# The last stage of a one-core attention and mixture-of-experts kernel: the output normalisation block by block, with roots by GpSimd and some sums by TensorE

## The chip, the cores and the metric

The kernel runs on one core of one Trainium2 chip. The metric is the device time of one execution in microseconds (us). A profiled execution also has a span, from the first to the last instruction of the program; all times inside a profile count from the start of the span. The engines are called PE (TensorE), DVE (VectorE), ACT (ScalarE), POOL (GpSimd) and SP (SyncE, which here only issues DMAs).

## The reference, cut to what matters

The input x is 4 x 1024 rows of 256 floats. After an attention layer with 16 heads comes a mixture of 8 experts, of which each row uses two; both layers stand between layer normalisations, and all is float32:

```python
x = x + _layernorm(_L0_attn_ref(_layernorm(x, axis=-1), ...), axis=-1)
x = x + _layernorm(_L0_ffn_ref(_layernorm(x, axis=-1), ...), axis=-1)
...
def _layernorm(x, axis=-1, eps=1e-05):
    m = jnp.mean(x, axis=axis, keepdims=True)
    v = jnp.var(x, axis=axis, keepdims=True)
    return (x - m) / jnp.sqrt(v + eps)
...
        h = jax.nn.silu(xs @ Wg[e] + bg[e]) * (xs @ W1[e] + b1[e])
        out = out + we[:, e:e + 1] * (h @ W2[e] + b2[e])
```

The change touches the last line of the first extract alone: the sum of a row's two weighted expert results, its layer normalisation, and the addition to the residual.

## The kernel before, in words

The attention fills the first two thirds of the span, with PE, DVE and ACT all at work; POOL takes part in the rotary embedding, in the small root calculations and in sending rows to their experts. Then the expert stage runs over 46 tiles of 256 or 128 rows. For each tile PE multiplies, ACT applies silu, DVE multiplies and scales (`up`, `down`), and POOL sends the weighted result by an indirect DMA (line 1276) to the DRAM tensor `res`, which has a place for the first and for the second expert's result of each row. PE's `pu` tiles of this stage lie in the PSUM pool `psu`, which has five buffers of one bank each.

When all results have landed, the end begins. The 4096 rows are eight blocks of 512. A block is an SBUF tile of 128 partitions, each with four rows; the four rows of a partition are called four tiles `t`.

1. `results` (line 1293) loads both results of each block into a tile `a` of its own: `a[:, 0]` on SP's queue, `a[:, 1]` on ACT's queue, half a megabyte each. All sixteen loads are issued first.
2. `scales_of` works on a pair of blocks: for each block DVE adds the two results (line 1302) and takes statistics of each tile (line 1304). `norm_scales` then makes mean and variance (line 358), adds eps (line 360) and calls `inverse_root`. That computes 1/sqrt(v) by an integer first guess (lines 337 and 338, always on DVE) and three Newton steps on the engine `e` it is given. On DVE a step is three instructions (lines 342 to 345), on POOL four. Two more instructions make the offset (lines 363 and 364). A root on DVE is so 11 instructions after the first guess, on POOL 14. Here `e` is DVE.
3. ACT scales each tile with the root and the offset (line 1310), from `a[:, 0]` into `a[:, 1]`.
4. `store` adds the residual (DVE, line 1317) and issues the store on SP (line 1318).

The engines SP, PE, DVE and ACT run in the order in which the program gives their instructions (a manual schedule), and POOL's instructions are kept in program order by the wrapper `InOrder` (line 328 is where they are all recorded). The order before is: statistics and roots of pair 0, of pair 1, stores of pair 0, pair 2, stores of pair 1, pair 3, stores of pair 2, stores of pair 3. The small tiles of the root (`mv`, `var`, `i`, `y`, `t`, `off`) have two buffers each.

Of the kernel before, what the change touches and what calls it, by code (L numbers as in the profile page):

```python
# [8 lines left out]
F32 = mybir.dt.float32  # L9
I32 = mybir.dt.int32  # L10
F32R = mybir.dt.float32r
AF = mybir.ActivationFunctionType
# [4 lines left out]
P = 128  # L17
B, T, C = 4, 1024, 256
# [6 lines left out]
NTB = TB // P  # L25
NBLK = B * T // TB
# [31 lines left out]
def sandwich(  # L58
# [4 lines left out]
    nc = tc.nc  # L63

    const = ctx.enter_context(tc.tile_pool(name="const", bufs=1))
    small = ctx.enter_context(tc.tile_pool(name="small", bufs=2))
# [65 lines left out]
    ident = const.tile([P, P], F32, tag="ident", name="ident")  # L132
# [34 lines left out]
    def compact():  # L167
        for i in range(2):
            for k in range(KC):
                nc.scalar.copy(  # L170
                    wqk[:, k, :, i],
                    w2x[:, i * KC + k, :].rearrange("p (g h d) -> p g h d", h=4, d=32)[..., :HD],
                )
# [117 lines left out]
    for e in range(NE):  # L291
        for w, to, cols in (
            (wg, 0, slice(0, FF)), (w1, FF, slice(FF - (P - R2), FF)), (w1, FF + P - R2, slice(0, NC * P))
        ):
            n = cols.stop - cols.start
# [34 lines left out]
    pool = InOrder(nc.gpsimd)  # L330

    def inverse_root(v, shape, name, e):

        i = small.tile(shape, I32, tag=f"ir{name[0]}", name=f"i_{name}")
        y = small.tile(shape, F32, tag=f"rt{name[0]}", name=f"y_{name}")
        t = small.tile(shape, F32, tag=f"rr{name[0]}", name=f"t_{name}")
        nc.vector.tensor_scalar(i, v.bitcast(I32), 1, None, ALU.arith_shift_right)
        nc.vector.tensor_scalar(  # L338
            y.bitcast(I32), i, -1.0, float(0x5F3759DF), ALU.mult, ALU.add
        )  # L340
        for _ in range(3):
            e.tensor_tensor(t, y, y, ALU.mult)
            if e is nc.vector:
                e.scalar_tensor_tensor(t, t, -0.5, v, ALU.mult, ALU.mult)
                e.scalar_tensor_tensor(y, t, 1.5, y, ALU.add, ALU.mult)
            else:
                e.tensor_tensor(t, t, v, ALU.mult)
                e.tensor_scalar(t, t, -0.5, 1.5, ALU.mult, ALU.add)
                e.tensor_tensor(y, y, t, ALU.mult)
        return y  # L350

    def norm_scales(stats, n, name, e=None):


        e = e or pool
        mv = small.tile([P, n, 2], F32, tag=f"mv{name[0]}", name=f"mv_{name}")
        for t in range(n):
            nc.vector.bn_aggr(mv[:, t, :], stats[:, t, :])
        v = small.tile([P, n], F32, tag=f"var{name[0]}", name=f"var_{name}")
        nc.vector.tensor_scalar(v, mv[:, :, 1], EPS, None, ALU.add)  # L360
        rstd = inverse_root(v, [P, n], name, e)
        off = small.tile([P, n], F32, tag=f"off{name[0]}", name=f"off_{name}")
        e.tensor_tensor(off, mv[:, :, 0], rstd, ALU.mult)
        e.tensor_scalar(off, off, -1.0, None, ALU.mult)
        return mv, rstd, off

    def normalized(out, src, scales, t):
        _, rstd, off = scales
        nc.scalar.activation(
            out, src, AF.Identity, bias=off[:, t : t + 1], scale=rstd[:, t : t + 1]  # L370
        )
# [5 lines left out]
    def stats_tile(name):  # L377
        return small.tile([P, NTB, 6], F32, tag=f"st{name[0]}", name=f"st_{name}")
# [19 lines left out]
    def bank_free(r, n):  # L398
        return max(ring[r][(taken[r] + i) % len(ring[r])] for i in range(n))
# [56 lines left out]
    def run_one(first="PADGW"):  # L456

        w = next((w for w in works if w.need[0] in first and w.fits()), None)
        if w:
            w.run()  # L460
        return w
# [623 lines left out]
    room = {}  # L1085
# [209 lines left out]
            )  # L1295
        return a

    def scales_of(pair):

        stats = small.tile([P, 2 * NTB, 6], F32, tag="st4", name=f"sto_{pair}")  # L1300
        for i, a in enumerate(sums[2 * pair : 2 * pair + 2]):
            nc.vector.tensor_tensor(a[:, 0], a[:, 0], a[:, 1], ALU.add)  # L1302
            for t in range(NTB):
                nc.vector.bn_stats(stats[:, i * NTB + t, :], a[:, 0, t, :])  # L1304
        scales = norm_scales(stats, 2 * NTB, f"o{pair}", nc.vector)
        for i, a in enumerate(sums[2 * pair : 2 * pair + 2]):
            for t in range(NTB):
                _, rstd, off = scales
                n = slice(i * NTB + t, i * NTB + t + 1)
                nc.scalar.activation(  # L1310
                    a[:, 1, t, :], a[:, 0, t, :], AF.Identity, bias=off[:, n], scale=rstd[:, n]
                )

    def store(blk, q):
        b, t0 = blk // 2, (blk % 2) * TB
        a = sums[blk]
        nc.vector.tensor_tensor(a[:, 1], a[:, 1], xs[blk], ALU.add)  # L1317
        q.dma_start(
            out=out[b, t0 : t0 + TB, :].rearrange("(p t) c -> p t c", p=P), in_=a[:, 1]
        )  # L1320

    sums, xs = [], []
# [29 lines left out]
    with tc.manual_schedule(engines={ET.SP, ET.PE, ET.DVE, ET.Activation}):  # L1352

        starts = [prepare(0, h, x_first[h], fast=True) for h in range(NQB)]
        for k in range(20):
            for gen in starts:
                next(gen, None)
            if k == 4:
                compact()
                small_constants()  # L1360
            if k == 8:
                turned_constants()
        plan_stacks()
        for h in range(NQB):
            splitting[0, 0, h].finish()
        for h in range(NQB):
            stacking[0, 0, h].finish()
        for t in range(NT):
            pressing.append(Work(values(0, [t]), t - 1))
        late = [Work(late_constants(), 40), Work(biases_by_chunk(), 57, start=54)]  # L1370
        while drawn[0] < UNIT:
            if bank_free("D", 2) <= free["P"]:
                peaks()
            elif not run_one():
                free["P"] = bank_free("D", 2)
        shifts[0].finish()
        for n in range(len(order) * NT):
            plan(n)
            for w in list(works):
                if w.due < n and w in pressing:  # L1380
                    w.finish()
            step(n)
            if "tb" not in room and n >= (len(order) - 4) * NT:

                if all(w.need is None for w in [*stacking.values(), *pressing]):
                    make_room_early()
                    first = Work(first_tiles(), n, after=[settling[divmod(NA - 1, NQB)]])
        while waiting:
            weighted(*waiting.pop(0))
        for to, of in bulk:  # L1390
            nc.sync.dma_start(out=to, in_=of)
        backs[-1].finish()
        first.finish()
        make_room()

        last = iter(())
        xT = transposed(0, ready[0][0])
        for j in range(MT):  # L1400
            if j == MA - 2:
                while works:
                    if not run_one():
                        free["P"] += 200
                for _ in other_tiles():
                    pass
            xt, w = ready.pop(0)
            for f in (NC, 0, 1):
                up(j, w, xT, f)
                run_one()  # L1410
            next(last, None)
            for f in (2, 3):
                up(j, w, xT, f)
                run_one()
            for _ in last:
                pass
            if j + 2 < MT:
                ready.append(fetch(j + 2))
            if j + 1 < MT:
                nxt = transposed(j + 1, ready[0][0])  # L1420
            up(j, w, xT, 4)
            xT, last = nxt, down(j, xt, w)
            if MA <= j < MA + NBLK:

                blk = j - MA
                xb = room["hp"].tile([P, NTB, C], F32, tag=f"x{blk}", name=f"x_{blk}")
                nc.sync.dma_start(
                    out=xb, in_=resid[blk * TB : (blk + 1) * TB, :].rearrange("(p t) c -> p t c", p=P)
                )
                xs.append(xb)  # L1430
        for _ in last:
            pass
        weights.close()
        open_pool("lp", behind, bufs=1, side="right")
        for blk in range(NBLK):
            sums.append(results(blk))
        for pair in range(NBLK // 2 + 1):
            if pair < NBLK // 2:
                scales_of(pair)
            if pair:  # L1440
                for i in range(2):
                    store(2 * pair - 2 + i, nc.sync)
    behind.close()


# [77 lines left out]
```

## Time and profile before

| what | value |
|---|---|
| median of 4 runs (lowest, highest) | 1680.26 us (1678.57, 1683.75) |
| the profiled execution's own time | 1680.44 us |
| its span | 1678.4 us |
| PE busy, share of the span | 1536.4 us, 92% |
| DVE busy | 1062.8 us, 63% |
| ACT busy | 853.7 us, 51% |
| POOL busy | 507.2 us, 30% |
| DMA, mean over the span | 147 GB/s |
| last indirect DMA of `down` issued | 1622.82 |
| first load of the end issued | 1625.23 |
| end of the last DVE instruction | 1674.85 |

The shares are means over stages with different limits. The end is some 53 us of the 1678, so it is read by itself: in the timeline (instructions in order of time, with the idle time before each), in windows (busy time of each engine in a stretch, with PE's granted clock), and in groups by line. A group's row gives the line, the engine, the operation, the tiles written and read, and the count, with the shortest, the median and the longest duration.

### The profile page before, as it was taken

How to read it: one execution, taken by the hardware profiler on the slowest of the kernel's cores; microseconds unless marked ns; L12 is line 12 of the kernel's file. 1: busy time of each engine (PE TensorE's matmuls, PEld its weight loads, DVE VectorE, ACT ScalarE, POOL GpSimd, SP SyncE). 2: the span in 40 equal slices, each digit the busy share in tenths (PEclk: the TensorE clock that was granted, in tenths of full speed). 3: DMA queues.
4: the chain of work that ended last, by engine and by line, in shares of the span. 5: the costliest groups of instructions: out<-in, count | busy, mean ns of one | idle time of the engine just before them, and what ended most of it. 6: DMA issues, size and time to landing. Idle time of an engine off the chain costs nothing. (4 is left out here: it accounts for less than half of the span.)

```text
span 1678.4 us, 27338 instructions
## 1 busy us (share of the span) xinstructions
PE 1536.4 (92%) x9448; PEld 1002.5 (60%) x9448; DVE 1062.8 (63%) x2535; ACT 853.7 (51%) x1753; POOL 507.2 (30%) x915
## 2 busy tenths in 40 slices
PE   3789999999989999999999999999999999999960
PEld 2344455654545554445554444788888888888850
DVE  6558778788688788778788894334434333333338
ACT  2156677676757677667677767422221111222213
POOL 5360262065354055265144121223230111111100
PEclk8879999999999999999999999999999999999985
DMA  2549769253434351204033032245455555778755
GB/s 79 144 117 275 204 188 271 58 140 95 128 75 98 89 173 40 63 26 103 15 82 81 1 118 102 77 166 203 159 194 191 205 202 199 266 281 288 286 204 209
DMA packets 102782, 247.32 MB, mean 147 GB/s; under 512 B 14029, under 2 KB 73652, under 8 KB 96756
## 3 DMA queue, kind: packets, MB, share of 16 engines
q1 hardware_dynamic: 92404, 215.00, 41.0%
q0 software_dynamic: 8768, 25.33, 4.7%
q10 hardware_dynamic: 1472, 5.24, 0.9%
q8 instruction: 75, 1.23, 0.3%
q14 instruction: 63, 0.52, 0.1%
HBM read 148.75 MB, written 80.58 MB: 137 GB/s over the span
## 5 line engine op out<-in xcount | busy, mean ns | idle before, releaser
L672 DVE TENSOR_REDUCE part<-pm 128x1 f32<-128x512 f32 x1024 | 640.3, 681 | 154.3 <-PE pm L668 153.2
L764 ACT ACTIVATE e<-sc 128x512 f32<-128x512 f32 x1024 | 529.7, 604 | 154.5 <-PE sc L760 153.2
L1229 PE MATMUL pu<-xT,w 128*128 128x256 f32 (+3 forms) x2024 | 361.7, 332 | 3.5 <-DVE xT L1211 1.0
L1229 PEld LDWEIGHTS pu<-xT,w 128*128 128x128 f32 (+1 forms) x2024 | 313.8, 189 | 36.6 <-issue 6.0
L1235 ACT ACTIVATE sil<-pu,w 128x256 f32<-128x256 f32 (+3 forms) x276 | 117.0, 424 | 429.5 <-PE pu L1229 400.9
L668 PE MATMUL pm<-stack,stack 64*128 64x512 f32 x960 | 273.8, 468 | 28.5 <-DVE part L672 14.5
L829 PE MATMUL av<-e,v 128*32 128x512 f32 x2048 | 276.8, 610 | 0.3 <-ACT e L764 0.3
L1240 DVE SCALAR_TENSOR_TENSOR h<-pu,w,sil 128x256 f32<-128x256 f32 (+1 forms) x230 | 97.1, 423 | 220.0 <-ACT sil L1235 219.8
L668 PEld LDWEIGHTS pm<-stack,stack 64*128 64x128 f32 x960 | 133.0, 186 | 169.7 <-DVE part L672 108.4
L760 PE MATMUL sc<-shift,bring 64*128 64x512 f32 x1024 | 224.5, 400 | 0.4 <-ACT shift L657 0.2
L753 PE MATMUL sc<-stack,stack 64*128 64x512 f32 x960 | 213.9, 408 | 9.1 <-ACT half L603 7.8
L1276 POOL DMA_INDIRECT res<-yo,ids x71 | 68.8, 969 | 427.4 <-DVE yo L1275 426.0
L1263 PE MATMUL pe<-w,h 128*128 128x256 f32 x710 | 169.6, 386 | 0.0
L1263 PEld LDWEIGHTS pe<-w,h 128*128 128x128 f32 x710 | 130.9, 190 | 31.1 <-issue 15.2
L753 PEld LDWEIGHTS sc<-stack,stack 64*128 64x128 f32 x960 | 111.5, 188 | 38.3 <-ACT half L603 12.9
L760 PEld LDWEIGHTS sc<-shift,bring 64*128 64x128 f32 x1024 | 108.1, 187 | 21.3 <-ACT shift L657 5.3
L1275 DVE TENSOR_SCALAR yo<-pe,xt 128x256 f32<-128x256 f32 x71 | 34.3, 483 | 99.9 <-PE pe L1263 99.9
L829 PEld LDWEIGHTS av<-e,v 128*32 128x32 f32 x2048 | 40.9, 108 | 71.7 <-issue 66.0
L1016 POOL DMA_INDIRECT rows<-xr,to x64 | 62.6, 978 | 60.9 <-DVE to L1011 26.8
L328 POOL TENSOR_TENSOR rot<-turned,bias_qk 128x512 f32<-128x512 f32 x31 | 40.9, 1319 | 115.2 <-ACT turned L528 108.1
L328 POOL TENSOR_TENSOR t_y<-y_y 128x4 f32<-128x4 f32 x24 | 4.7, 197 | 187.3 <-DVE y_y L338 186.1
L523 PE MATMUL pp<-wqk,nT 128*128 128x512 f32 (+1 forms) x128 | 61.0, 600 | 0.0
(293 smaller groups left out, 1418.8 us busy)
## 6 DMA issues: line engine op xcount, KB each, us to landing
w<-wall SPq DMA_DIRECT2D x46, 2034.0 KB
rows<-empty SPq DMA_DIRECT2D x35, 1032.0 KB
stack<-half SPq DMA_DIRECT2D x92, 256.0 KB
stack<-half SPq DMA_DIRECT2D x64, 128.0 KB
xt<-rows SPq DMA_DIRECT2D x25, 258.0 KB
wall<-in_wg_dram SPq DMA_DIRECT2D x16, 342.0 KB
wall<-in_w_dram SPq DMA_DIRECT2D x16, 320.0 KB
wall<-in_w_dram SPq DMA_DIRECT2D x8, 640.0 KB
```

The costliest lines, as they stand in the source:

```text
L668: nc.tensor.matmul(pm, q[r, t * P : (t + 1) * P], k_[r, half * TB : (half + 1) * TB], start=True, stop=True,)
L672: nc.vector.tensor_reduce(part[:, i, 2 * pr + s, half : half + 1], pm, AX.X, ALU.max)
L753: nc.tensor.matmul(sc, k_[r, kb * P : (kb + 1) * P], q[r, qb * TB : (qb + 1) * TB], start=True, stop=False,)
L760: nc.tensor.matmul(scs[s], bring[pr][r, :], shift[u][r, :], start=False, stop=True)
L764: nc.scalar.activation(e, scs[s], AF.Exp, scale=1.0 / HD**0.5)
L829: nc.tensor.matmul(av[32 * j : 32 * j + 32, :], v_aug[kb][:, 4 * g + j, :], es[j], start=(kb == 0), stop=(kb == NT - 1),)
L1016: sent = nc.gpsimd.indirect_dma_start(out=rows[:, :], out_offset=bass.IndirectOffsetOnAxis(ap=to[:, i, t : t + 1], axis=0), in_=xr[:, t, i ...
L1229: nc.tensor.matmul(pu[:m, i, :n], w[:, c0 : c0 + m], xT[:, k, :n], start=(k == 0), stop=(k == KC - 1),)
L1235: nc.scalar.activation(sil[:m, :n], pu[:m, 0, :n], AF.Silu, bias=w[:m, OB + f : OB + f + 1])
L1240: nc.vector.scalar_tensor_tensor(h[:, f, :n], pu[:, 1, :n], bias, sil[:, :n], ALU.add, ALU.mult)
L1263: nc.tensor.matmul(po[:, :C], hs[j % 2][:, f, i * P : (i + 1) * P], w[:, O2 + f * C : O2 + (f + 1) * C], start=False, stop=(f == NC - 1),)
L1276: sent = nc.gpsimd.indirect_dma_start(out=res[:, :], out_offset=bass.IndirectOffsetOnAxis(ap=ids, axis=0), in_=y, in_offset=None,)
```

## The change

The end goes block by block. In `summed_up`, for blocks 1, 3 and 5, PE sums the two results: for each half of the block (two tiles, 512 columns) two products with the identity matrix are accumulated into a PSUM bank of the pool `psu`, and the statistics and ACT's scaling then read PSUM. For the other five blocks DVE adds as before. Each block has its own `norm_scales`; the roots of blocks 0 to 6 go to POOL, that of block 7 stays on DVE. The store of block k - 2 is placed after the statistics of block k and ahead of its aggregates and root. The last two stores follow at the end. Loads, stores and their queues are as they were.

```diff
-    def scales_of(pair):
-
-        stats = small.tile([P, 2 * NTB, 6], F32, tag="st4", name=f"sto_{pair}")
-        for i, a in enumerate(sums[2 * pair : 2 * pair + 2]):
+    def summed_up(blk):
+
+        a, by_tile = sums[blk], []
+        if blk in (1, 3, 5):
+            for n in range(2):
+                p = room["psu"].tile([P, 2, C], F32, tag="pu", name=f"sum_{blk}_{n}")
+                for i in range(2):
+                    nc.tensor.matmul(
+                        p.rearrange("p t c -> p (t c)"), ident,
+                        a[:, i, 2 * n : 2 * n + 2].rearrange("p t c -> p (t c)"),
+                        start=(i == 0), stop=(i == 1),
+                    )
+                by_tile += [p[:, 0], p[:, 1]]
+        else:
             nc.vector.tensor_tensor(a[:, 0], a[:, 0], a[:, 1], ALU.add)
-            for t in range(NTB):
-                nc.vector.bn_stats(stats[:, i * NTB + t, :], a[:, 0, t, :])
-        scales = norm_scales(stats, 2 * NTB, f"o{pair}", nc.vector)
-        for i, a in enumerate(sums[2 * pair : 2 * pair + 2]):
-            for t in range(NTB):
-                _, rstd, off = scales
-                n = slice(i * NTB + t, i * NTB + t + 1)
-                nc.scalar.activation(
-                    a[:, 1, t, :], a[:, 0, t, :], AF.Identity, bias=off[:, n], scale=rstd[:, n]
-                )
+            by_tile = [a[:, 0, t] for t in range(NTB)]
+        stats = stats_tile(f"o{blk}")
+        for t in range(NTB):
+            nc.vector.bn_stats(stats[:, t, :], by_tile[t])
+        return by_tile, stats
+
+    def scaled(blk, by_tile, scales):
+        for t in range(NTB):
+            normalized(sums[blk][:, 1, t], by_tile[t], scales, t)
...
-        for pair in range(NBLK // 2 + 1):
-            if pair < NBLK // 2:
-                scales_of(pair)
-            if pair:
-                for i in range(2):
-                    store(2 * pair - 2 + i, nc.sync)
+
+        for blk in range(NBLK):
+            by_tile, stats = summed_up(blk)
+            if blk > 1:
+                store(blk - 2, nc.sync)
+            scales = norm_scales(stats, NTB, f"o{blk}", pool if blk < NBLK - 1 else nc.vector)
+            scaled(blk, by_tile, scales)
+        for blk in (NBLK - 2, NBLK - 1):
+            store(blk, nc.sync)
```

`normalized` is the same ACT instruction that `scales_of` used, and `stats_tile` gives a tile for the statistics of four tiles.

## The prediction

> **What bounds the kernel now.** I read the page first (spans and clock), then the timeline of the last 60 us, then the waits of that stretch, then earlier stretches for the prices of what is new. The part that the change touches begins when the last results have landed in DRAM. In the timeline the columns are start, length, engine, line, operation, count, and in brackets the idle time before and what ended it.
>
> ```profile
> 1625.24 14.45 ACTq L1293 DMA_DIRECT2D a<-res  x8
> 1630.64 1.23 DVE L1302 TENSOR_TENSOR a<-a 128x1024 f32<-128x1024 f32 x1 [8.09 <-DMA a<-res]
> 1631.90 1.41 DVE L1304 BATCH_NORM_STATS2 sto<-a 128x6 f32<-128x256 f32 x4
> 1633.47 1.22 DVE L1302 TENSOR_TENSOR a<-a 128x1024 f32<-128x1024 f32 x1 [0.17 <-DMA a<-res]
> ...
> 1669.56 4.04 ACT L1310 ACTIVATE a<-a,off_o,y_o 128x256 f32<-128x256 f32 x8 [6.72 <-DVE off_o L364]
> 1673.63 1.22 DVE L1317 TENSOR_TENSOR a<-a,x 128x1024 f32<-128x1024 f32 x1 [0.72 <-ACT a L1310]
> ```
>
> The reader sees one engine: DVE starts at 1630.64 when block 0 lands and works until 1674.85 with two short waits. The windows by stage agree; their columns are busy times of PE, PEld, DVE, ACT and POOL, then clock, DMA share, GB/s:
>
> ```profile
> 1640.00:1650.00 10.00, 0.00 (x0) 0.00 (x0) 9.45 (x34) 5.74 (x12) 0.00 (x0) 0.50 0.79 313
> 1650.00:1660.00 10.00, 0.00 (x0) 0.00 (x0) 9.45 (x35) 3.29 (x8) 0.00 (x0) 0.50 0.26 104
> ```
>
> DVE is busy 9.45 of 10 us, POOL and PE not at all, and PE's granted clock has dropped to 0.50. The loads keep the DMA full (about 410 GB/s) until 1647.5, some 2.6 us a block; after that DMA is no bound. From the last add's end at 1674.85 to the span's end at 1678.4 are 3.55 us of store and shutdown, which stay. The execution's own time is 1680.44, 2.04 over its span; the median is 1680.26, so I add the difference to the median.
>
> **What leaves DVE.** By the timeline's pitches a DVE block costs: add 1.25, four statistics 1.33, four aggregates 0.33, three small operations (var, i, y) 0.60; the rest of a root 11 x 0.20 = 2.2; the result add before a store 1.19. Before: 8 x (1.25+1.33+0.33+1.19) + 4 x 14 x 0.20 = 44. After: five blocks at 1.25+1.33, three at 4 x 0.345 = 1.38 (statistics from PSUM have no row; of 128x256 operations with a PSUM input L706 took 424 ns and L1275 483, where L951 from SBUF took 425, so a tile costs 0 to 58 ns more, in all at most 0.7 us; I take 0.345 a tile, by L706, which is as much of a two-input read), eight times 0.33+0.60+1.19, one root of 2.2: 36.2. So 8 us leave DVE. I do not credit them, since three other things become late.
>
> **Late thing 1: the sums on PE.** Block 1 has four calls of 128x512. Line 194 shows that one fp32 call of that shape is two records, 1.02 us at full clock, so 0.5 a record.
>
> ```profile
> 25.79 1.02 PE L194 MATMUL pbias<-diag,ones 128*128 128x512 f32 x2
> 51.78 1.65 PE L523 MATMUL pp<-wqk,nT 128*128 128x384 f32 x2
> ...
> 53.00:54.00 1.00, 1.00 (x3) 0.50 1.05 340
> 54.00:55.00 1.00, 1.00 (x5) 0.82 1.06 329
> ```
>
> At half clock two records of 384 columns took 1.65, so one of 512 takes 1.65/2 x 512/384 = 1.1. A burst that began at 51.05 got the full clock at 54.36 (0.82 in that microsecond is 36% at 0.50), after 3.3 us. PE starts at 1633.5: three records by 1636.8, five at 0.5, and 0.15 to the reader: the second half is there at 1639.45. DVE, done with block 0 at 1634.1, takes tiles 0 and 1 at 1637.2 and the other two until 1640.15; aggregates and small operations end at 1641.1. DVE has stood still for 4.7 us. Bounds: 5.0 without any waiting (the sum could not be earlier than the load), and 6.9 when the clock stays at 0.50 for all eight records (8 x 1.1 + 0.15). Blocks 3 (landed about 1639.3) and 5 (about 1644.2) are summed long before DVE asks for them, and stay so at half clock within 1.5 us.
>
> [...]
>
> **Late thing 2: POOL is slower and is held up.** A root of 14 operations took POOL 433.24 to 437.10, 3.86 us (DVE: 2.2). It never ran beside DVE's big SBUF adds in this kernel, and the new end puts ten of those adds beside it. The nearest rows are those where both engines did two-input work in SBUF:
>
> ```profile
> 27.51 1.79 POOL L328 TENSOR_TENSOR rot<-turned,bias_qk 128x512 f32<-128x512 f32 x1 [7.00 <-ACT bias_qk L197]
> ...
> 31.10 1.59 POOL L328 TENSOR_TENSOR rot<-rot,turn 128x512 f32<-128x512 f32 x1
> ...
> 27.46 0.69 DVE L550 TENSOR_TENSOR rot<-turned,bias_qk 128x512 f32<-128x512 f32 x1 [0.79 <-ACT bias_qk L197]
> ...
> 30.48 1.09 DVE L561 TENSOR_TENSOR rot<-rot,turn 128x512 f32<-128x512 f32 x1
> ...
> L328 POOL TENSOR_TENSOR rot<-turned,bias_qk x31: 1261/1305/1789, 27.5 to 853.4; 128x512 f32<-128x512 f32 x31
> L328 POOL TENSOR_TENSOR rot<-rot,turn x31: 1260/1282/1591, 31.1 to 856.3; 128x512 f32<-128x512 f32 x31
> ```
>
> The first POOL operation began with 0.64 us of DVE's left and took 1.79 for a median 1.305: 0.48 lost, the rest less 0.16. The second had 0.47 left and lost 0.31: again the rest less 0.16. So POOL stands still while such a DVE operation runs. An add of 1.216 at some point in a chain costs it 1.216 - 0.16 - 0.05 (the gap between POOL's operations): 1.0. Bounds: 0 (none of the rows is of a 0.2 us operation behind a 1.2 us one) and 1.22. I take 1.0, since both rows give the same rule. In return DVE waits at most for the rest of a 0.2 us operation, a few hundredths. Statistics and aggregates hold nothing: roots beside L375 and L358 kept a pitch of 0.28 to 0.30.
>
> [...]
>
> **Late thing 3: one chain per block.** DVE's store add of block k-2 stands before the root of block k, so it now waits for POOL and ACT, and behind it queue the aggregates, the small operations and all later DVE work. ACT itself is free only at 1639.69 (its loads, first fence), which covers root 0. A block's scaling is four tiles: 0.585 + 3 x 0.49 = 2.1. The order from there (16xx us; POOL goes from chain to chain without a gap, since each y is ready before POOL is; a chain is 3.86 plus 1.0 for each add that falls into it):
>
> | root | POOL from | adds in it | to | scaled |
> |---|---|---|---|---|
> | 1 | 41.15 | add 2, store 0 | 47.0 | 49.1 |
> | 2 | 47.0 | store 1, add 4 | 52.9 | 55.0 |
> | 3 | 52.9 | store 2 | 57.7 | 59.8 |
> | 4 | 57.7 | store 3, add 6 | 63.6 | 65.7 |
> | 5 | 63.6 | store 4, add 7 | 69.5 | 71.6 |
> | 6 | 69.5 | store 5 | 74.3 | 76.4 |
>
> Six chains of 3.86 and ten adds of 1.0 are 33.2 us. Each store add starts when "scaled" says, so DVE idles 1 to 2 us before each. Block 7 is rooted on DVE by 1676.1 (y at 1673.8 and 2.2); ACT comes to it after block 6 and ends at 1678.4, and the last add at 1679.7. That is 4.85 after 1674.85: a span of 1683.2, the execution 1685.3, and on the median **1685.1 us**. Stores are issued on SP behind the loads (last issue 1639) and cost nothing; PE's sixth PSUM tile waits for the first to be read (five buffers), at about 1649, and block 5 is asked for at 1657.
>
> **Rivals.**
> 1. POOL and DVE don't hold each other in 0.2 us pieces. Then DVE paces: from 1641.1 blocks 2, 4, 6 at 4.7, blocks 3, 5 at 3.5, block 7 at 4.7+2.2, 28.0 in all, and 0.4 of waits: 1669.5; scaling 2.1 and the last add 1.25: 1672.9, which is 1.9 less, 1678.4. For it: small POOL operations kept their pitch beside DVE's PSUM work. Against: the rows above. It decides where a hold costs under about 0.5: each tenth less takes ten times 0.1 from the 4.85. With 0.6 to 0.8 a hold the time is 1681 to 1683.
> 2. No hold, and PE's sums ready when block 1 lands: then ACT's queue is next, store 0 can't start before 1639.7 + 2.1 = 1641.8, and y of block 2 comes at 1644.0 for 1645.8: another 1.8 less, -3.7, **faster**, 1676.5. Against: 0.50 in every window from 1625.
> 3. The clock does not rise, or holds are 1.22 each: +7.1 (the first term 2.3 later) or +7, about 1687.5.
> 4. The holds are there and PE's sums are no wait: root 1 then starts when root 0 ends (1634.2 + 3.9 = 1638.1), 3.0 sooner than in the table: +1.85, 1682.1.
>
> **Numbers.** Forecast (1683.7 to 1686.5) 0.42; rival 3 0.20; holds of 0.5 to 0.8 or rival 4 (1680.5 to 1683.6) 0.19; rival 1 0.12; rival 2 0.07. The range leaves out rival 2 and the far end of 3: 1678.3 to 1688.5. A measurement of this kernel tells about 0.2% (3.4 us) from no change. Slower by more: 0.62 and a little of the third case, 0.64; within: 0.29; faster: 0.07.
>
> **What would show it.** Right: DVE's first statistics of block 1 wait 3 to 4 us for PE, and the next pair again; POOL's root operations show lengths up to about 1.2 us, two of 14 in a chain; store adds wait for ACT by 1 to 2 us; POOL has no gap from 1641 to 1674. Wrong: roots of 3.9 us each, and DVE without gaps after 1641 (rival 1), or a clock of 1.00 before 1635 (rival 2).

## The result, and the profile after

The changed kernel takes 1684.13 us (median of 44 runs, 1681.18 to 1688.41) where the kernel before, measured beside it, takes 1680.7 us (66 runs, 1677.43 to 1688.21). The ratio is 1.0018, with a 95% interval from 1.0013 to 1.0024: slower by 2.2 to 4.0 us. The prediction took 0.2% (3.4 us) as the least that can be told from no change; the point lies just under that and the interval reaches over it, but 1.0000 lies well outside the interval.

The profiled execution took 1686.87 us, span 1685.1. Only part of that is the change: the stages ahead of it are the same code and differ by some microseconds from execution to execution (the first load of the end is issued at 1625.23 in the profile of before, at 1629.24 in this one, and at 1623.22 to 1628.04 in the profiles of e1 to e4 below). So I use one measure for all profiles, the **end stage**: from the issue of that first load to the end of the span. Before it is 1678.4 - 1625.23 = 53.2 us, after 1685.1 - 1629.24 = 55.9 us: 2.7 us longer, in agreement with the ratio (2.2 to 4.0).

The timeline after, as for before (start, length, engine, line, operation, count, idle time before it):

```profile
1634.66 1.23 DVE L1312 TENSOR_TENSOR a<-a 128x1024 f32<-128x1024 f32 x1 [8.10 <-DMA a<-res]
...
1637.01 5.10 PE L1305 MATMUL sum<-a,ident 128*128 128x512 f32 x8 [10.97 <-DMA a<-res]
...
1640.43 0.76 DVE L1316 BATCH_NORM_STATS2 st_o<-sum 128x6 f32<-128x256 f32 x2 [2.21 <-PE sum L1305]
...
1642.15 0.76 DVE L1316 BATCH_NORM_STATS2 st_o<-sum 128x6 f32<-128x256 f32 x2 [0.96 <-PE sum L1305]
...
1643.71 1.23 DVE L1312 TENSOR_TENSOR a<-a 128x1024 f32<-128x1024 f32 x1
...
1643.89 1.11 POOL L328 TENSOR_TENSOR t_o<-y_o 128x4 f32<-128x4 f32 x1 [1.71 <-DVE y_o L338]
...
1645.07 0.20 POOL L328 TENSOR_TENSOR t_o<-t_o,var_o 128x4 f32<-128x4 f32 x1
...
1646.29 1.21 DVE L1326 TENSOR_TENSOR a<-a,x 128x1024 f32<-128x1024 f32 x1
...
1646.48 1.08 POOL L328 TENSOR_SCALAR t_o<-t_o 128x4 f32<-128x4 f32 x1
...
1651.54 1.23 DVE L1326 TENSOR_TENSOR a<-a,x 128x1024 f32<-128x1024 f32 x1 [1.80 <-ACT a L369]
...
1651.74 1.08 POOL L328 TENSOR_TENSOR t_o<-y_o 128x4 f32<-128x4 f32 x1
...
1676.21 4.04 ACT L369 ACTIVATE a<-a,off_o,y_o 128x256 f32<-128x256 f32 x8 [2.78 <-POOL off_o L328]
...
1680.28 1.23 DVE L1326 TENSOR_TENSOR a<-a,x 128x1024 f32<-128x1024 f32 x1 [0.75 <-ACT a L369]
```

Three things are to be seen. DVE waits 2.21 and 0.96 us for PE's two halves of block 1. Each DVE add (1643.71, 1646.29, 1651.54) has a POOL operation beside it that takes 1.1 us instead of 0.2 and ends with the add. And DVE's add before a store waits 1.80 us for ACT, which waits for POOL. The windows (PE, PEld, DVE, ACT, POOL busy, clock, DMA share, GB/s) show the bound changing hands:

```profile
1650.00:1660.00 10.00, 1.98 (x4) 0.68 (x4) 7.16 (x23) 3.58 (x8) 7.96 (x26) 0.85 0.49 196
1660.00:1670.00 10.00, 0.00 (x0) 0.00 (x0) 7.45 (x25) 4.01 (x8) 7.95 (x27) 0.50 0.22 86
```

DVE falls from 9.45 of 10 us to 7.2 to 7.5, while POOL, idle before, works without a pause (its 0.2 us operations stand 0.28 apart, and the gaps don't count as busy). The groups of the root's tile `t_o` give the price of a hold, that is of one add beside which POOL stands still (shortest/median/longest ns):

```profile
L328 POOL TENSOR_TENSOR t_o<-y_o x21: 197/198/1222, 1638.3 to 1673.7; 128x4 f32<-128x4 f32 x21
L328 POOL TENSOR_SCALAR t_o<-t_o x21: 192/193/1078, 1638.9 to 1675.1; 128x4 f32<-128x4 f32 x21
```

Ten of POOL's 98 operations are stretched, to 1.13 us on average, each beside one of the ten adds that the prediction's table lists, and in the same order. Ten times (1.13 - 0.20) is 9.3 us of POOL standing still.

### The profile page after: what moved, and what is told of

Read it like the earlier page. It is cut to its first block, busy times and chain, and to the rows that moved or that the text cites. A ratio compares the mean times of both kernels' runs of the same rounds, so it can differ in the third digit from the quotient of the medians.

```text
span 1685.1 us, 27486 instructions
## 1 busy us (share of the span) xinstructions
PE 1553.4 (92%) x9472; PEld 1009.2 (60%) x9472; DVE 1057.1 (63%) x2511; ACT 853.8 (51%) x1753; POOL 535.7 (32%) x1013
## 3 DMA queue, kind: packets, MB, share of 16 engines
q8 instruction: 75, 1.23, 0.3%
## 5 line engine op out<-in xcount | busy, mean ns | idle before, releaser
L1016 POOL DMA_INDIRECT rows<-xr,to x64 | 62.6, 978 | 61.9 <-DVE to L1011 28.0
```

The costliest lines, as they stand in the source:

```text
L1016: sent = nc.gpsimd.indirect_dma_start(out=rows[:, :], out_offset=bass.IndirectOffsetOnAxis(ap=to[:, i, t : t + 1], axis=0), in_=xr[:, t, i ...
```

## The experiments

Theory: POOL stands still while DVE runs an add with two inputs in SBUF; this makes the chain of roots the bound, and PE's late sum of block 1 shifts its start. Rivals: the handing from engine to engine is the cost, whatever POOL's lengths; or the late sum alone; or POOL is slowed by any DVE work. All lengths are of the end stage in the profile (before 53.2, after 55.9), the ratios are to the kernel before on the same chip. The four kernels e5 to e8 ran on a chip where the kernel before takes 1705.08 us, for 1680.54 to 1680.78 with the others; there too only ratios and end stages are compared. Their first adds (5.39 to 5.53 us after the first load's issue) and the length of an add (1.22 us) are as with the others.

There is one profile for each kernel. From the issue of the first load to DVE's first add pass 5.22 to 5.74 us in these twelve profiles, so half a microsecond between two end stages means nothing, and the 1 us of e6 and e8 is weak by itself. By the runs e3, e6 and e8 can't be told from the changed kernel (the intervals overlap).

| kernel | end stage, us | stretched POOL operations | ratio to before (95%) |
|---|---|---|---|
| e1: stores from PSUM | 51.4 | 4 | 0.9988 (0.9978 to 0.9998) |
| e2: roots by DVE | 62.6 | none | 1.0045 (1.0028 to 1.0061) |
| e3: sums by DVE | 57.9 | 13 | 1.0029 (1.0019 to 1.0039) |
| e4: pairs, three sums by PE | 50.7 | none | 0.9992 (0.9982 to 1.0002) |
| e5: no holds | 53.6 | 1 | 0.9997 (0.9983 to 1.0011) |
| e6: adds split | 54.9 | 16 | 1.0002 (0.9985 to 1.0019) |
| e7: pairs, six sums by PE | 51.7 | none | 0.9982 (0.9968 to 0.9996) |
| e8: PE kept warm | 54.8 | 10 | 1.0014 (0.9996 to 1.0032) |
| e9: pairs, four sums, PE warm | 48.0 | none | 0.9980 (0.9970 to 0.9991) |
| e10: few holds | 50.3 | 3 | 0.9984 (0.9975 to 0.9993) |

**e1: the store adds read PSUM.** ACT's scaled tiles go to PSUM; DVE's adds are the same sums with one input moved.

```diff
-            normalized(sums[blk][:, 1, t], by_tile[t], scales, t)
+                normalized(p[:, t], by_tile[2 * n + t], scales, 2 * n + t)
...
-        nc.vector.tensor_tensor(a[:, 1], a[:, 1], xs[blk], ALU.add)
+            nc.vector.tensor_tensor(a[:, 1, ts], out_ps[blk][n], xs[blk][:, ts], ALU.add)
```

> ACT writes the scaled tiles to PSUM, so that the six store adds beside POOL's roots (two adds of 512 columns each) have only one input in SBUF. Hold theory (POOL stands still while DVE runs an add with two inputs in SBUF): those adds no longer stretch any POOL operation, six of ten holds of about 0.93 us go, chains of 4.8 us at most, and the end gets 4 to 5 us shorter than in the changed kernel, 1 to 1.5 us under the kernel before. Rival (the time goes into handing each block from DVE to POOL to ACT to DVE, whatever POOL's lengths): the end stays within 0.7 us of the changed kernel. Second rival (POOL is slowed by any DVE work): the stretched operations stay.

Measured: 4.4 us shorter than the changed kernel, with four stretched operations, one beside each of the adds 2, 4, 6 and 7. DVE even waited 1 us longer for PE (2.75 and 1.48 us for 2.21 and 0.96). The timeline of e1 at the place where the changed kernel has its second stretched operation:

```profile
1641.32 0.20 POOL L328 TENSOR_TENSOR t_o<-t_o,var_o 128x4 f32<-128x4 f32 x1
1641.42 1.27 DVE L1332 TENSOR_TENSOR a<-scaled,x 128x512 f32<-128x512 f32 x2
1641.61 0.19 POOL L328 TENSOR_SCALAR t_o<-t_o 128x4 f32<-128x4 f32 x1
1641.89 0.20 POOL L328 TENSOR_TENSOR y_o<-y_o,t_o 128x4 f32<-128x4 f32 x1
1642.16 0.20 POOL L328 TENSOR_TENSOR t_o<-y_o 128x4 f32<-128x4 f32 x1
```

POOL runs three operations at full pace while DVE adds from 1641.42 to 1642.69. The last rival (any DVE work) is out, and so is the first: the handing over is as in the changed kernel, and 4.4 us are gone. The late sum alone, the middle one, doesn't fit either: DVE's two waits for it were longer here, and the end was earlier.

**e6: the control for e1.** The same split of the store adds, both inputs in SBUF.

```diff
-        nc.vector.tensor_tensor(a[:, 1], a[:, 1], xs[blk], ALU.add)
+        for n in range(2):
+            ts = slice(2 * n, 2 * n + 2)
+            nc.vector.tensor_tensor(a[:, 1, ts], a[:, 1, ts], xs[blk][:, ts], ALU.add)
```

> Control for e1: the store adds are split in two of 512 columns as there, but both inputs stay in SBUF. Hold theory: POOL is held twice for half as long, about 16 stretched operations (four long ones, twelve of 0.5 to 0.7 us), the end within 1 us of the changed kernel. Rival (e1 gained by the shorter adds, not by the input in PSUM): within 1 us of e1, 4 us under the changed kernel.

Measured: 54.9, 0.9 us under the changed kernel, with 16 stretched operations of 0.74 us on average; 16 x (0.74 - 0.20) = 8.6 us of standing still for 9.3. The timeline of e6 at the same store:

```profile
1669.81 0.20 POOL L328 TENSOR_TENSOR t_o<-t_o,var_o 128x4 f32<-128x4 f32 x1
1669.92 1.27 DVE L1328 TENSOR_TENSOR a<-a,x 128x512 f32<-128x512 f32 x2
1670.10 0.55 POOL L328 TENSOR_SCALAR t_o<-t_o 128x4 f32<-128x4 f32 x1
1670.73 0.52 POOL L328 TENSOR_TENSOR y_o<-y_o,t_o 128x4 f32<-128x4 f32 x1
```

DVE's row is as long as in e1 (1.27 us); POOL gets two operations done in place of more than four. So it is the place of the input, not the length of the add. A hold as long as the whole add would cost 1.22 us, an estimate from the add's own length; in the changed kernel it cost 0.93, since the held operation began 0.06 to 0.20 us after the add, ended some 0.05 us after it, and would have taken 0.20 us anyway.

**e2: all roots on DVE; e3: all sums on DVE.** Each undoes one part.

```diff
-            scales = norm_scales(stats, NTB, f"o{blk}", pool if blk < NBLK - 1 else nc.vector)
+            scales = norm_scales(stats, NTB, f"o{blk}", nc.vector)
```

> The changed kernel with all eight roots on DVE: POOL's part undone alone. Hold theory: DVE takes 7 x 2.2 = 15.4 us more and has nothing to wait for, so the end is set by DVE alone: 36.2 + 15.4 = 51.6 us of DVE work against 44 before, some 10 us slower than before, 7 slower than the changed kernel. Rival (POOL is simply the wrong engine): faster than the changed kernel.

```diff
-        if blk in (1, 3, 5):
+        if blk in ():
```

> The changed kernel with all eight sums on DVE: PE's part undone alone. Hold theory: no wait for PE in block 1 (3.2 us less), but three more adds (3.75 us of DVE) that hold POOL too, so 1 us slower than the changed kernel, some 4 us slower than before. Rival (the late PE sum of block 1 is what costs): 2 to 3 us faster than the changed kernel, equal to before.

Measured: e2 is 9.4 us longer than before and 6.8 longer than the changed kernel (expected 10 and 7). Roots block by block are eight roots for the four of before, and POOL takes seven of them; held up as it is, it still beats DVE doing them. e3 is 2.0 us longer than the changed kernel (expected 1), with 13 stretched operations, three more than with PE's sums; up to 0.3 us of the 2.0 is a later landing of the first load. By the profiles the sums by PE are worth having, though block 1's comes late; the rival (the late sum is what costs) is out.

**e8: PE kept warm.** Twelve idle products, results unread, between the last expert tile and the landing of the loads.

```diff
+        for i in range(12):
+            p = bank(f"warm_{i}")
+            nc.tensor.matmul(
+                p, ident, xs[0][:, 0:2].rearrange("p t c -> p (t c)"), start=True, stop=True
+            )
```

> The changed kernel with twelve idle products on PE between the last expert tile and the landing of the loads, results unread, to keep PE's clock up. Clock theory: the granted clock is 1.00 when block 1 lands, its second half is summed 3.7 us after the landing (5.1 in the changed kernel), root 1 starts 1.4 us sooner and the whole end is 1.4 us shorter; POOL is held as before. Rival (DVE's wait for block 1 is hidden behind POOL and ACT): no change.

Measured: 54.8, 1.1 us shorter than the changed kernel (expected 1.4); root 1 starts 13.3 us after the first load's issue, for 14.65. The timeline of e8 shows PE summing block 1 in 3.67 us where the changed kernel took 5.10, and DVE waiting 1.7 us where it waited 3.2:

```profile
1645.56 10.46 PE L1444 MATMUL warm<-x,ident 128*128 128x512 f32 x24
1656.76 3.67 PE L1305 MATMUL sum<-a,ident 128*128 128x512 f32 x8 [0.74 <-DMA a<-res]
```

**e4 and e7: PE's part without POOL.** The order and the DVE roots of the kernel before; the sums of blocks 3, 5, 7 (e4) or 2 to 7 (e7) by PE.

```diff
+            blk = 2 * pair + i
+            if blk in (3, 5, 7):
+                for n in range(2):
+                    p = room["psu"].tile([P, 2, C], F32, tag="pu", name=f"sum_{blk}_{n}")
...
+            else:
+                nc.vector.tensor_tensor(a[:, 0], a[:, 0], a[:, 1], ALU.add)
```

> The order and the DVE roots of the kernel before, with the sums of blocks 3, 5 and 7 by PE: PE's part alone, and no POOL. My theory: DVE loses three adds of 1.25 and waits for nothing, since each sum is there before DVE asks (block 3 lands about 14 us after the first load's issue, DVE asks 17 us after it), so 3 to 3.8 us faster than before. Rival (statistics from PSUM or a cold PE eat it): within 1 us of before.

> The order and DVE roots of the kernel before, the sums of blocks 2 to 7 by PE (six PSUM halves in the one pool, six in the other). My theory: DVE loses 6 x 1.25 = 7.5 us and waits 2 to 3 us for the sums of blocks 2 and 3, which PE makes at half clock: 4.5 to 5.5 us faster than before. Rival (PE or its PSUM banks become the bound): no faster than the 50.7 us from the first load's issue that three sums took.

Measured: e4's end stage is 2.5 us shorter than before; three adds gave 3.75, and 1.1 went to waits for block 3 on a cold PE (0.18 and 0.95), one that begins its sums at a granted clock of 0.50. That is short of the 3 to 3.8 expected, and its runs' interval includes no change. e7, with six adds less, is 1.5 us shorter only, and misses its 4.5 to 5.5: DVE waits for PE six times, 5.5 us. Two of its rows:

```profile
1667.99 0.76 DVE L1318 BATCH_NORM_STATS2 sto<-sum 128x6 f32<-128x256 f32 x2 [0.95 <-PE sum L1308]
...
1681.21 0.76 DVE L1318 BATCH_NORM_STATS2 sto<-sum 128x6 f32<-128x256 f32 x2 [1.40 <-PE sum L1308]
```

Four of the waits (3.3 us) are in blocks 2 and 3: there PE, even at full clock, brings a half every 1.72 us, and DVE's statistics of a half take 0.76. The last two (2.1 us) come after PE in its turn has waited for ACT (3.0 us), because the PSUM banks are still being read. So the rival (PE or its banks become the bound) is right there, in both its parts. By the runs e4 and e7 can't be told apart (their intervals overlap); the end stages of the profiles can.

**e5: nearly no holds, and a new wait.** e1 with the sums of blocks 2 to 7 by PE.

```diff
-        if blk in (1, 3, 5):
+        if blk in (2, 3, 4, 5, 6, 7):
```

> The kernel of e1 (store adds read PSUM) with the sums of blocks 2 to 7 by PE, blocks 0 and 1 by DVE: add 1 is the only add with two inputs in SBUF beside a root. Hold theory: one stretched operation (in root 0, before ACT is free anyway), roots of 3.9 us, and the end about 4.9 us shorter than in the kernel before, 8 shorter than in the changed kernel. Rival (some other cost of POOL roots): not under the 51.4 us from the first load's issue that e1 took.

Measured: 53.6, a clear miss; expected were 48.3, and the rival (not under 51.4) stood. One operation was stretched as foreseen, but twelve halves go through five banks. The timelines of e5:

```profile
1674.80 8.83 PE L1305 MATMUL sum<-a,ident 128*128 128x512 f32 x16 [2.88 <-ACT scaled L369]
...
1678.52 0.76 DVE L1316 BATCH_NORM_STATS2 st_o<-sum 128x6 f32<-128x256 f32 x2 [4.76 <-PE sum L1305]
```

PE's sum of block 4 can't begin its second half before ACT has scaled block 2 out of that bank, and DVE waits 4.76 us for it, and 11.4 us for PE in all. Not all of that is the bank: PE, idle for 2.9 us, fell back to half clock (0.50 in the window from 1675 to 1678) and its four records took 3.5 us, where a half at full clock takes 1.7. The first two waits (3.25 us) are block 2's sum on a PE that was cold at its start. My expectation had left the number of banks out.

**e9 and e10: the two lessons in one kernel each.** e10 is e1 with PE's sums for blocks 2, 3, 5, 6, so that the bank is free again in time. e9 is the order of before with DVE roots, PE's sums for blocks 3, 4, 5, 7 in banks of both pools, and sixteen idle products. First e10's edit against e1, then the start of e9's against the kernel before:

```diff
-        if blk in (1, 3, 5):
+        if blk in (2, 3, 5, 6):
```

```diff
+            if blk in (3, 4, 5, 7):
...
+        for i in range(16):
+            p = bank(f"warm_{i}")
...
```

> The kernel of e1 with PE's sums for blocks 2, 3, 5 and 6, so that no half waits for a bank; the adds of blocks 1, 4 and 7 stay on DVE beside roots 0, 3 and 6. Hold theory: three stretched operations, no wait for PE in block 1 and one of 2 us in block 2, about 3.3 us faster than before: 49.5 to 50.5 us from the first load's issue. Rival (what e5 lost was not the wait for PSUM banks but POOL's roots themselves): no better than e1's 51.4.

> The order and DVE roots of the kernel before, the sums of blocks 3, 4, 5 and 7 by PE in PSUM banks that are free when they are asked for (three blocks in the one pool, one in the other), and sixteen idle products that keep PE's clock up until the loads land. My theory (DVE's work sets the end, and PE's sums are free where neither its clock nor its banks make them late): four adds of 1.25 less, no wait for PE over 1 us in all, 4 to 5 us faster than before, 48.2 to 49.2 us from the first load's issue to the end for 53.2. Rival (six sums gave no more than three, so PE's sums have a limit of their own at about 50.7 us): not under 50.5.

Measured: e10 50.3 and three stretched operations, inside its range; DVE waited 3.8 us for PE's cold sum of block 2, and 0.33 for a bank. So by the profiles POOL's roots are not themselves what cost in e5. e9 took 48.0, 5.2 us shorter than before (expected 4 to 5) and 7.8 shorter than the changed kernel. It has the lowest ratio, 0.9980, but the runs give it only 1.5 to 5.0 us over the kernel before, and its interval overlaps those of e1, e4, e5, e7 and e10. Windows of e9:

```profile
1642.00:1652.00 10.00, 10.00 (x24) 4.29 (x23) 9.50 (x37) 6.80 (x15) 0.00 (x0) 1.00 0.92 367
1652.00:1662.00 10.00, 2.40 (x6) 0.76 (x4) 9.49 (x36) 3.83 (x9) 0.00 (x0) 0.87 0.34 134
```

DVE is as full as before (9.5 of 10), but with four adds less to do, and it waits for PE nowhere. e9 changes the clock, the banks and the number of sums at once, so it doesn't tell what each of them is worth.

## Why the prediction was right, and where it was too large

The forecast was slower by 4.85 us; measured are 2.2 to 4.0 by the runs and 2.7 by the profiles. Counted from the issue of the first load (1625.23 in the prediction's times, 1629.24 in the profile after):

| step | predicted | measured |
|---|---|---|
| first half of block 1's sum read by DVE | 12.0 | 11.2 |
| second half read | 14.2 | 12.9 |
| root 1 starts on POOL | 15.9 | 14.65 |
| root 6 ends | 49.1 | 46.9 |
| last add ends | 54.5 | 52.3 |
| end | 58.0 | 55.9 |

- **What leaves DVE** was right in its place: 36.2 us of pitches for 44, and as busy time 34.9 for 41.2. It bought nothing, as said; DVE idled instead.
- **Late thing 1** was right as a mechanism (e8) and 1.3 us too long, which is more than half the excess. Two of its terms were off. "PE starts at 1633.5" is 8.3 us after the issue; PE began 7.77 us after it, 0.5 sooner, since its first product reads only the half that SP's queue loads, where DVE's add before needed both halves (8.24). And "one of 512 takes 1.1" and "0.5 a record" were too long: the products' records, by their weight loads, stand 0.85 us apart at half clock and 0.43 at full clock. My two rows were short runs of two records, and the second record's tail was counted as pitch: the two of line 194 are 0.594 us long on average and overlap, 1.02 us in all. From PE's start until DVE read the second half 5.1 us passed, for 5.95.

```profile
1638.85 0.34 PEld L1305 LDWEIGHTS sum<-a,ident 128*128 128x128 f32 x1 [0.52 <-issue]
1639.70 0.29 PEld L1305 LDWEIGHTS sum<-a,ident 128*128 128x128 f32 x1 [0.52 <-issue]
...
1640.66 0.19 PEld L1305 LDWEIGHTS sum<-a,ident 128*128 128x128 f32 x1 [0.24 <-issue]
1641.09 0.19 PEld L1305 LDWEIGHTS sum<-a,ident 128*128 128x128 f32 x1 [0.24 <-issue]
```

- **The clock rose sooner here than in e1 and e2.** In this profile it rose 2.9 us after the products began (1.00 in the window from 1640 to 1641, 0.55 in the one before) where I took 3.3. In e1 and e2 PE began the same sum equally soon (7.74 and 7.76 us after the issue), and the clock rose 4.7 and 4.4 us later (0.54 in e1's window from 1635 to 1636, 0.80 in the same window of e2). DVE's two waits were 4.2 us in e1, for 3.2. With e1's clock the end would come about 1 us later and closer to the forecast, an estimate from these two profiles; what the other runs of the changed kernel had is not on record. The rise in the profile after (columns: length, PE busy, clock, DMA share, GB/s):

```profile
1639.00:1640.00 1.00, 1.00 (x3) 0.55 1.01 410
1640.00:1641.00 1.00, 1.00 (x3) 1.00 1.03 414
```

- **The bounds of late thing 1** do not follow from its terms. Eight records of 1.1 us put the second half 3.0 us later, not 2.3, so rival 3 should have read 7.9 in place of 7.1; the lower bound of 5.0 stands above the 4.7 that it seems to bound; and tiles 0 and 1, after four records, come at 1637.45 and not at 1637.2. The sum that gives the forecast uses none of the three.
- **Late thing 2**: the ten holds came where the table has them. A hold cost 0.93 us for the 1.0 that I took (the rule from the two rows, the rest of the add less 0.16, held: 1.05 - 0.16 for the first, which lost 0.91); six chains and ten holds took 32.3 us for 33.2. That is the other part of the excess. e1 and e6 show the condition, both inputs of the add in SBUF (16 stretched operations in e6, 4 in e1); why POOL stands still then, no run shows.
- **Late thing 3**: the store adds waited for ACT by 0.92 to 1.80 us, and POOL went from chain to chain without a gap, as written. From root 6's end to the last add's end 5.3 us passed, for 5.4.
- **Rivals**: without holds between small operations (rival 1) falls by the stretched operations themselves, PE's sums ready with the load (rival 2) by DVE's 3.2 us of waits for them, and the far case (rival 3) by the clock that rose and by the 0.93 a hold. PE's sums as no wait (rival 4) was priced at 3 us less; e8, which takes 1.5 of the 3.2 us of wait away, gained 1.1.

The terms that were too large sum to 1.3 + 0.9 = 2.2 us, and 4.85 - 2.2 is the 2.65 of the profiles.

## What to carry to other kernels

Before work is moved to GpSimd, list the VectorE instructions with two SBUF inputs that will run beside it: here each add of 1.22 us cost the GpSimd chain 0.93 us, while VectorE lost next to nothing (1.21 to 1.23 us an add, 1.217 before), and a chain of many short GpSimd operations then paces the loop. With one input of the store adds in PSUM 4 GpSimd operations were stretched, with both in SBUF 16 (e1 against e6). Sums as identity products are cheap for the engine that is full, if TensorE's clock is kept up (block 1's sum took 3.67 us in e8, 5.10 in the changed kernel), if the next sum is not asked for sooner than TensorE can bring it (a half of a block every 1.72 us at full clock), and if the PSUM banks are counted against the time that each stays in use (e9 for e7 and e5). A wait for a bank can cost twice: in e5 TensorE stood idle for 2.9 us, and the half that followed, at a clock of 0.50, took 3.5 us, for 1.7 at full clock.

## What the runs showed of the hardware that was not expected

- DVE paid next to nothing for the holds, less than the few hundredths that the prediction allowed: its adds took 1.21 to 1.23 us beside POOL, for 1.217 before on average. The first three operations of root 7 on DVE ran beside POOL's last two, and all kept their usual lengths (0.16 and 0.21 to 0.22 us).
- The same code met a different clock: the rise came 2.9, 4.4 and 4.7 us after the same products began (the changed kernel, e2, e1).
- An ACT scaling of four tiles took 1.93 us out of PSUM and 2.07 out of SBUF.
- Idle products cost no time that the profiles show: with 10.5 us of them (e8) DVE waited 8.2 us for its first loads, 8.09 before. With 13.9 us of them (e9) the granted clock was 1.00 in the windows from 1622 to 1642, and PE's first sum began at 1640.32; the kernel before has 0.50 from 1625 on.
